# A cross-attention prologue re-ordered: query projections moved into the first units' steps, loads re-sequenced, key transfers on a second queue, feature maps in two pieces

## The chip, the cores and the metric

The kernel runs on one core of a Trainium2 chip. A core has a matrix engine (PE, whose weight loads the profile shows as PEld), a vector engine (DVE), a scalar engine (ACT), a general engine (POOL) and SyncE (SP), which here only issues transfers. Each works through its own instructions in order; semaphores tie them together. PE writes into eight PSUM banks, which DVE and ACT read out. The metric is the device time of one execution in microseconds, smaller is better.

## The reference

One layer over x (4 batches, 256 rows, 256 columns) with a context of 4 x 4096 rows. All in float32:

```python
x = x + xattn(layernorm(x), ctx, ctx)    # 16 heads of 16: softmax(Q K^T / 4) V, then Wh
x = x + attn(layernorm(x))               # causal, features exp(clip(x_n @ omega * sqrt(2s) - s))
x = x + ffn(layernorm(x))                # silu(gate) * up, then down; hidden 768
```

Nearly all the work is the first line: for each of 4 x 16 heads 256 queries meet 4096 keys.

## The kernel before

`cross_attention` works in 16 **units**: a batch and a quad of four heads. A unit has 16 **steps**; a step takes 256 keys. In step n of the main loop (L1116) PE makes transposed scores (`pt`, L856), ACT takes their exponential (`e`, L861), and the product with the values (`pav`, L876) follows one step behind; DVE adds it up (L886). The softmax needs a maximum for each query row first. These come from a second set of scores (`pm`, L810), whose row maxima DVE takes (L817), for the unit after the present one; at a unit's end `shift` (L821) negates the maxima and puts them into a row of the query tile, so that the exponential is taken of shifted scores. Beside this each step makes half a chunk of keys (`pk`, L188) or values (`pv`, L188) for a later unit: `key` and `value` (L736, L763) project 512 context rows. A key chunk leaves PSUM through ACT (`ku`, L753) and is spread by eight small transfers (L756, 16 partitions each) over two of three key tiles `kts`, at rows 32 apart. Those tiles are filled with ones beforehand, since a row of ones meets the shift row.

The first unit has no earlier unit to take its maxima in. The **prologue** (L990 to L1099) makes up for it: it loads weights and context, makes keys 0 to 7 of the first head pairs, values 0 to 3, and runs 16 groups `g` of four `pm` with their maxima, with three more groups for the unit after (`extra`, L1084). `behind` (L1064) says what PE and ACT do after each group. Before it come the queries: `queries(b)` (L939) has a layernorm, a `turn` (four transposes and two copies), for batch 0 a `project` of its first two quads straight into `qT`, and `spread(m)` for half of the quads, which goes through a tile `qu` (L980) and eight transfers on POOL's queue (L983). All of it is done in the prologue for every batch. `qT` is cleared by POOL (L990, L991), and POOL fills the whole of `va`, the later attention's values, with ones (L458). Eleven matmuls of a unit matrix (L1011) stand at the start.

On PE, ACT, DVE and SP the order is the program's own, written out by hand (`manual_schedule`). POOL's order comes from the planner. Each transfer of SP or ACT takes one of eight completion semaphores in turn and waits for the transfer that had it before.

The last unit's steps carry the start of the causal attention (`plan`, L495): `features(n)` (L301) makes a quad's feature maps by PE (`pf`, L309), DVE (clip, L315), ACT (exponential, L316) and POOL (a factor on the key half, L317). `attend` (L321) uses them for masked scores `pa`, their product `po` with `va` and a division. After the last unit a hand-made list (L643 to L672) interleaves the remaining attention with the feed-forward: `hidden(m)` (L576) makes a gate product `pg` and an up product `pu`.

Of the kernel before, what the change touches and what calls it, by code (L numbers as in the profile page):

```python
# [20 lines left out]
P = 128  # L21
# [18 lines left out]
def perceiver_layer(  # L40
# [32 lines left out]
    def load_queries():  # L73

        for to, src, queue in ((bk_sb, bkP, nc.scalar), (bqu_sb, bqP, nc.gpsimd)):
            for q in range(NQ):
                queue.dma_start(
                    out=to[64 * (q % 2) : 64 * (q % 2) + 64, q // 2 : q // 2 + 1],
                    in_=src.rearrange("(j r) q -> j r q", r=32)[:, 1 : 1 + HD, q : q + 1],
                )  # L80
        nc.scalar.dma_start(out=wq_sb, in_=wqP)
        nc.scalar.dma_start(out=bq_sb, in_=bqP)

# [217 lines left out]
    def features(n):  # L301
# [11 lines left out]
        for i, pf in enumerate(pfs):  # L313
            f = feature(n + i // 2, i % 2)
            nc.vector.tensor_scalar(f, pf.rearrange("p s t -> p (s t)"), low, top, ALU.max, ALU.min)  # L315
            nc.scalar.activation(f, f, AF.Exp, bias=shift)  # L316
            nc.gpsimd.tensor_scalar(f[:, T:], f[:, T:], fac, 1.0, ALU.mult, ALU.mult)  # L317

# [125 lines left out]
    def start_causal():  # L444
# [10 lines left out]
        def constants():  # L455


            nc.gpsimd.memset(va, 1.0)  # L458
# [29 lines left out]
        def call(f, *args):  # L488
# [21 lines left out]
            -3: [call(features, 0)],  # L510
            -1: [steps[0][0]],
            0: [steps[0][1], steps[1][0]],
            1: [call(features, 2)],
            2: [steps[1][1], call(qk_normed, 2)],
# [6 lines left out]
            9: [call(features, 4)],  # L521
            10: [project_o],
# [13 lines left out]
        tc, xr, load_x, load_queries, load_rest, ctxT, wq_sb, bq_sb, bqu_sb, wkP, bk_sb, wvP, eps, ident, layernorm, product4,  # L536
# [22 lines left out]
    def feed_forward(b):  # L559
# [15 lines left out]

        def hidden(m):  # L576
            pg, pu = bank([P, 2, T], "pg"), bank([P, 2, T], "pu")
            for ps, w in ((pg, wg), (pu, wu)):
                for i in range(2):
                    ns = slice((2 * m + i) * P, (2 * m + i + 1) * P)  # L580
                    for k in range(KC):
                        nc.tensor.matmul(  # L582
                            ps[:, i, :], lhsT=w[:, k, ns], rhs=zT[:, k, :], start=k == 0, stop=k == KC - 1
                        )
            th = work.tile([P, 2, T], F32, tag="th", name="th")
            nc.scalar.activation(th, pg, AF.Tanh, scale=0.5)
            nc.vector.scalar_tensor_tensor(th, th, 1.0, pg, ALU.add, ALU.mult)
            nc.vector.tensor_tensor(hT[:, 2 * m : 2 * m + 2, :], pu, th, ALU.mult)
# [18 lines left out]
        return norm, turn, hidden, down  # L607

    with tc.manual_schedule(engines={ET.PE, ET.Activation, ET.DVE, ET.SP}):
# [52 lines left out]
        for n in range(NQ, NB + 1):  # L662
            if n > NQ + 1:
                steps[n - 1][1]()
            if NQ < n < NB:
                steps[n][0]()
            for piece in first.get(n, []):
                piece()
# [6 lines left out]
def cross_attention(tc, xr, load_x, load_queries, load_rest, ctxT, wq_sb, bq_sb, bqu_sb, wkP, bk_sb, wvP, eps,  # L675
# [17 lines left out]
    nc = tc.nc  # L693
    NU = B * NQ
# [3 lines left out]
    with ExitStack() as st:  # L698
# [15 lines left out]
        ones = big.tile([P, 1], F32, tag="ones", name="ones")  # L714

# [223 lines left out]
        def queries(b):  # L939
# [7 lines left out]
            def turn():  # L947
# [3 lines left out]
                for i in range(2):  # L951
# [3 lines left out]
                    nc.scalar.copy(  # L955
# [4 lines left out]
            def project():  # L960

                for i in range(2):
                    ps = bank([P, T], "pq")
                    for k in range(KC):
# [3 lines left out]
                    nc.scalar.activation(  # L968
                        qT[:, i, b * T : (b + 1) * T], ps, AF.Identity, bias=bq_sb[:, i : i + 1]
# [19 lines left out]

        nc.gpsimd.memset(qT[:, 2:, :T], 0.0)  # L990
        nc.gpsimd.memset(qT[:, :, T:], 0.0)  # L991
        with tc.manual_schedule(engines={ET.PE, ET.Activation, ET.DVE, ET.SP}):
            nc.sync.dma_start(out=wk, in_=wkP.rearrange("p k (h r) -> p k h r", r=32))
            for b in range(1, B):
                load_context()
                load_x(b)
            nc.sync.dma_start(out=wv, in_=wvP)

# [3 lines left out]
            load_queries()  # L1002
            nc.vector.tensor_reduce(ones, ident.rearrange("p (j r) -> p r j", r=32)[:, 0, :], AX.X, ALU.add)

            def fill(kt, c0, c1, engine=nc.vector):
                engine.tensor_copy(kt[:, c0 * CH : c1 * CH], ones.to_broadcast([P, (c1 - c0) * CH]))


            warm = bank([P, P], "warm")
            for _ in range(11):  # L1010
                nc.tensor.matmul(warm, lhsT=ident, rhs=ident, start=True, stop=True)  # L1011
# [7 lines left out]
            for i in range(2):  # L1019
                fill(kts[i], 0, 2)  # L1020
            normal = [q[0]() for q in qs]
            for piece in normal[0]:
                piece()
            headed(wk, wk_sb)
            qs[0][1]()
            for i in range(2):
                fill(kts[i], 2, NCH)
            normal[1][0]()
            whole(key(0, 0, (nc.sync, nc.scalar) * 2 + (nc.sync,) * 4))
            qs[0][2]()  # L1030
            for piece in normal[1][1:]:
                piece()
# [3 lines left out]
            nc.vector.memset(neg0, 0.0)  # L1036
            whole(key(0, 1))
            wqu = wide.tile([P, KC, 2 * D], F32, tag="wk", name="wqu")
            headed(wq_sb.rearrange("p k (h r) -> p k h r", r=32), wqu[:, :, :D])
            for k in range(KC):  # L1040
                nc.scalar.copy(
                    wv_sb[:, k, :].rearrange("p (h d) -> p h d", d=HD),
                    wv[:, k, : H * (HD + 1)].rearrange("p (h e) -> p h e", e=HD + 1)[:, :, :HD],
                )

            def filled(c):
                return lambda: nc.scalar.copy(
                    kts[2][:, 2 * c * CH : 2 * (c + 1) * CH], ones.to_broadcast([P, 2 * CH])
                )

            def keys(c):
                return lambda: whole(key(0, c))
# [174 lines left out]
```

## Time and profile before

| | |
|---|---|
| median of three runs | 1184.65 us (1183.34 to 1185.9) |
| the profiled execution | 1184.44 us |
| its span, first to last instruction | 1182.7 us |
| granted PE clock over the span | 0.997 |
| PE busy | 1171.0 us (99%) |
| DVE busy | 904.8 us (77%) |
| ACT busy | 696.5 us (59%) |
| POOL busy | 236.8 us (20%) |
| chain that ended last, by engine | PE 97%, DVE 2%, ACT 1% |
| DVE row maxima L817 | 1024, 683 ns each, 634.9 us |
| query transfers L983 on POOL | 56, 486 ns an issue, 3.7 us to landing |

The span is the time between the first and the last instruction of the program; the execution's time is a little longer. An engine's busy time is the union of its instructions. In the timeline and the groups, a row names the line, the operation, `out<-in`, the shapes and how many instructions it merges; float32 matmuls appear as two records each, so 16 `pk` matmuls are 32 records. In square brackets stands the engine's idle time before the row and what released it. PE's matmuls overlap in the array, so a run's length is best read from the start of one run to the start of the next.

### The profile page before, as it was taken

The page shows a single profiled execution, that of the slowest core. Times are in us where ns is not written, and L with a number is a line of the kernel's source. Part 1 is how long each engine was busy: PE and PEld are TensorE (multiplying, and loading weights), DVE is VectorE, ACT ScalarE, POOL GpSimd, SP SyncE. Part 2 cuts the span into 40 slices and gives each one's busy share as a digit, 9 for nine tenths or more (in the row PEclk, how much of TensorE's full clock was granted, in tenths as well). Part 3 has the DMA queues.
Part 4 walks back from the last instruction along what each step waited for, and adds up shares of the span by engine and source line. Part 5 has one row for each costly group of instructions (what it writes and reads, how often), then busy time and mean ns, then how long its engine had stood idle before and what let it go on. Part 6 is the DMA issues. An engine that isn't in the chain of part 4 may idle for free.

```text
span 1182.7 us, 42980 instructions
## 1 busy us (share of the span) xinstructions
PE 1171.0 (99%) x18024; PEld 798.5 (68%) x18024; DVE 904.8 (77%) x1723; ACT 696.5 (59%) x1444; POOL 236.8 (20%) x443
## 2 busy tenths in 40 slices
PE   8999999999999999999999999999999999999998
PEld 4476667766776677667766776667666666667777
DVE  7987787777777777877777877798887788567753
ACT  4456666666666655666666665666664456876442
POOL 3730302011111212120202020303031132213210
PEclk8999999999999999999999999999999999999999
DMA  6562442234223432333224322432233112000000
GB/s 211 145 208 66 115 121 81 61 103 114 85 78 87 118 96 74 81 111 101 83 76 117 93 80 75 113 113 83 66 105 111 39 42 69 11 2 10 10 11 18
DMA packets 55160, 99.99 MB, mean 85 GB/s; under 512 B 23392, under 2 KB 28056, under 8 KB 54968
## 3 DMA queue, kind: packets, MB, share of 16 engines
q1 hardware_dynamic: 44904, 91.84, 26.2%
q0 software_dynamic: 9440, 4.81, 2.1%
q8 instruction: 143, 2.34, 0.8%
q10 hardware_dynamic: 624, 0.59, 0.2%
q14 instruction: 49, 0.40, 0.1%
HBM read 76.13 MB, written 3.21 MB: 67 GB/s over the span
## 4 chain that ended last, share of the span: by engine, by line
PE 97%; DVE 2%; ACT 1%; issue 0%; POOL 0%; ACTq 0%; POOLq 0%
PE pt L856 23%; PE pm L810 19%; PE pav L876 19%; PE pv L188 11%; PE pk L188 11%; PE pg L582 2%; PE pd L598 2%; PE pu L582 2%; PE pa L335 1%; PE pqk L188 1%; PE po L361 1%; DVE mx L817 1%; PE py L409 1%; PE pf L309 1%; PE py L188 1%; PE pa L340 1%
## 5 line engine op out<-in xcount | busy, mean ns | idle before, releaser
L861 ACT ACTIVATE e<-pt 128x512 f32<-128x512 f32 x1024 | 529.3, 602 | 374.4 <-PE pm L810 356.6
L817 DVE TENSOR_REDUCE mx<-pm 128x1 f32<-128x512 f32 x1024 | 634.9, 683 | 127.0 <-PE pm L810 126.7
L856 PE MATMUL pt<-qa,kt 32*128 32x256 f32 x4096 | 501.4, 388 | 0.7 <-DVE qa L842 0.5
L810 PE MATMUL pm<-kt,qT 32*128 32x512 f32 x2048 | 498.4, 617 | 0.1
L856 PEld LDWEIGHTS pt<-qa,kt 32*128 32x128 f32 x4096 | 318.0, 184 | 124.0 <-ACT v L781 42.4
L876 PE MATMUL pav<-e,v 128*32 128x256 f32 x4096 | 269.1, 380 | 0.0
L810 PEld LDWEIGHTS pm<-kt,qT 32*128 32x128 f32 x2048 | 181.3, 191 | 15.7 <-DVE mx L817 4.9
L876 PEld LDWEIGHTS pav<-e,v 128*32 128x32 f32 x4096 | 128.5, 110 | 74.0 <-issue 4.6
L886 DVE TENSOR_TENSOR av<-pav,av 128x256 f32<-128x256 f32 x240 | 101.6, 423 | 57.8 <-PE pav L876 57.3
L188 PE MATMUL pv<-wv_sb,wff 128*32 128x128 f32 x4096 | 137.3, 276 | 0.0
L188 PE MATMUL pk<-wff,wk_sb 128*32 128x256 f32 x2048 | 137.1, 389 | 0.0
L188 PEld LDWEIGHTS pv<-wv_sb,wff 128*32 128x32 f32 x4096 | 104.3, 109 | 43.1 <-DVE mx L817 43.1
L188 PEld LDWEIGHTS pk<-wff,wk_sb 128*32 128x32 f32 x2048 | 54.7, 110 | 66.6 <-DVE mx L817 38.8
L925 POOL TENSOR_TENSOR oT<-oT,bvT 128x64 f32<-128x64 f32 x32 | 8.6, 290 | 357.8 <-DVE oT L922 356.2
L908 POOL DMA_DIRECT2D oT<-scr x112 | 66.5, 626 | 22.1 <-DMA scr<-av 19.0
L753 ACT ACTIVATE ku<-pk,bk_sb 128x256 f32<-128x256 f32 x128 | 63.2, 495 | 12.6 <-PE pk L188 11.1
L832 POOL DMA_DIRECT2D qa<-neg x60 | 33.1, 564 | 133.8 <-DVE neg L829 96.3
L781 ACT COPY v<-pv 128x256 f32<-128x256 f32 x128 | 51.3, 401 | 9.7 <-PE pv L188 9.7
L352 DVE TENSOR_TENSOR at<-pa,mask 128x384 f32<-128x384 f32 x34 | 17.3, 551 | 19.5 <-PE pa L340 19.5
L983 POOL DMA_DIRECT2D qT<-qu x56 | 26.8, 486 | 14.6 <-ACT qu L980 11.1
L316 ACT ACTIVATE kt<-kt,shift 128x512 f32<-128x512 f32 x32 | 22.3, 727 | 8.4 <-DVE kt L315 8.4
L315 DVE TENSOR_SCALAR kt<-pf,low,top 128x512 f32<-128x512 f32 x32 | 23.7, 803 | 4.4 <-PE pf L309 4.3
(146 smaller groups left out, 645.3 us busy)
## 6 DMA issues: line engine op xcount, KB each, us to landing
wff<-in_ctxT_dram SPq DMA_DIRECT2D x128, 512.0 KB
kt<-ku SPq DMA_DIRECT2D x510, 32.0 KB
scr<-av POOLq DMA_DIRECT2D x14, 128.0 KB, 2.1
oT<-scr POOLq DMA_DIRECT2D x112, 8.0 KB, 2.7
xr<-in_x_dram SPq DMA_DIRECT2D x4, 256.0 KB
out_dram<-o SPq DMA_DIRECT2D x8, 128.0 KB
qa<-neg POOLq DMA_DIRECT2D x60, 1.0 KB, 3.5
qT<-qu POOLq DMA_DIRECT2D x56, 16.0 KB, 3.7
```

Source lines behind the costliest of these rows:

```text
L188: nc.tensor.matmul(out[js], lhsT=lhsT[:, js], rhs=rhs, **flags)
L582: nc.tensor.matmul(ps[:, i, :], lhsT=w[:, k, ns], rhs=zT[:, k, :], start=k == 0, stop=k == KC - 1)
L753: nc.scalar.activation(ku[:, cs], made.pop(), AF.Identity, bias=bk_sb[:, m : m + 1])
L781: nc.scalar.copy(to.rearrange("p t (h d) -> p t h d", d=HD + 1)[:, :, :, :HD], made.pop().rearrange("p t (h d) -> p t h d", d=HD),)
L810: nc.tensor.matmul(pm, lhsT=qT[rows, q, ts], rhs=kt[rows, c * CH : (c + 1) * CH], start=True, stop=True,)
L817: nc.vector.tensor_reduce(mx[:, i, j, c : c + 1], pm, AX.X, ALU.max)
L832: nc.gpsimd.dma_start(out=qa[32 * j : 32 * j + 1, :].rearrange("o (p i) -> o p i", i=2), in_=neg[:, j, :])
L856: nc.tensor.matmul(pt[:, i, :], lhsT=kt[rows, ks], rhs=qa[rows, :], start=True, stop=True)
L861: nc.scalar.activation(e, pt, AF.Exp, scale=0.25)
L876: nc.tensor.matmul(pav[32 * h : 32 * h + 32, :], lhsT=v[:, t % KT, c0 : c0 + 32], rhs=es[n, h][:, i, :], start=i == 0, stop=i == 1,)
L886: nc.vector.tensor_tensor(avs[u], pav, avs[u], ALU.add)
L908: queue.dma_start(out=oT[:, k, q % 2, j], in_=scr[32 * j : 32 * j + HD, k * P : (k + 1) * P].rearrange("e (r a) -> r e a", a=16),)
```

## The change

In the prologue:

- The transfers are issued in another order and on other queues. wq goes from ACT's queue to SP's. Of x and the context only what the first two key chunks use stands ahead of the first keys' transfers; x of batches 2 and 3, the value weights and later context chunks follow between the key chunks. Keys 2 to 7 put two of their eight transfers on POOL's queue.
- POOL no longer clears `qT`; ACT copies a column of zeros into it in pieces. DVE fills the key tiles with ones only for chunks 0 to 3; ACT fills the rest. `va` gets its ones by two DVE memsets of its columns of ones, in the step where POOL's memset stood in the plan.
- Batch 0's transposed layernorm and its first queries are read out by DVE instead of ACT. Twelve matmuls of the unit matrix stand at the start, and six more after key chunk 1.
- The statistics of batches 2 and 3 move by a group, and `behind` is dealt out anew; values 0 to 3 follow groups 11 to 14.

In the main loop, the second half of batch 0's queries and the turns and both halves of batches 1 to 3 stand after steps 1, 3 to 5, 7 to 9 and 17 to 19. `att0` takes its buffer when it is first used, since the query weights keep that buffer until then.

In the causal part, `features` becomes `feature_arguments` (PE, DVE) and `feature_exps` (ACT, POOL); in the plan of the last unit the second piece comes a step later. In the end phase one gate product is made ahead of the last unit's division.

```diff
@@ -70,16 +70,27 @@
     bk_sb, bqu_sb = (const.tile([P, KC], F32, tag=name, name=name) for name in ("bk_sb", "bqu_sb"))
-    def load_queries():
...
-        nc.scalar.dma_start(out=wq_sb, in_=wqP)
+    def load_biases():
+        load_spread(bk_sb, bkP, nc.scalar)
         nc.scalar.dma_start(out=bq_sb, in_=bqP)
+    def load_spread(to, src, queue):
...
+    def load_weights():
+        nc.sync.dma_start(out=wq_sb, in_=wqP)
+    def load_later():
+        nc.vector.memset(bqu_sb, 0.0)
+        load_spread(bqu_sb, bqP, nc.gpsimd)
+    loads = load_x, load_biases, load_weights, load_later
     bvT = const.tile([P, H], F32, tag="bvT", name="bvT")
...
@@ -298,7 +309,7 @@
         i = 2 * (n % 4) + part
         return kts[2 if n % 8 < 4 else 0][:, i * 2 * T : (i + 1) * 2 * T]
-    def features(n):
+    def feature_arguments(n):
         b, q = divmod(n, NQ)
         cs = slice(b * T, (b + 1) * T)
@@ -311,10 +322,19 @@
                     start=True, stop=True,
                 )
         for i, pf in enumerate(pfs):
+            nc.vector.tensor_scalar(
+                feature(n + i // 2, i % 2), pf.rearrange("p s t -> p (s t)"), low, top, ALU.max, ALU.min
+            )
+    def feature_exps(n):
+        for i in range(4):
             f = feature(n + i // 2, i % 2)
-            nc.vector.tensor_scalar(f, pf.rearrange("p s t -> p (s t)"), low, top, ALU.max, ALU.min)
             nc.scalar.activation(f, f, AF.Exp, bias=shift)
             nc.gpsimd.tensor_scalar(f[:, T:], f[:, T:], fac, 1.0, ALU.mult, ALU.mult)
+    def features(n):
+        feature_arguments(n)
+        feature_exps(n)
     got, place = [], {}
...
@@ -455,7 +475,8 @@
         def constants():
-            nc.gpsimd.memset(va, 1.0)
+            nc.vector.memset(va[:, :, : H * (HD + 1)].rearrange("p t (h e) -> p t h e", e=HD + 1)[:, :, :, HD], 1.0)
+            nc.vector.memset(va[:, :, H * (HD + 1) :], 1.0)
             nc.vector.tensor_scalar(top, rest[6], 20.0, None, ALU.add)
             nc.vector.tensor_scalar(low, rest[6], -20.0, None, ALU.add)
             nc.vector.tensor_scalar(shift, rest[6], -1.0, None, ALU.mult)
...
@@ -507,19 +528,20 @@
...
-            -3: [call(features, 0)],
+            -3: [call(feature_arguments, 0)],
+            -2: [call(feature_exps, 0)],
             -1: [steps[0][0]],
             0: [steps[0][1], steps[1][0]],
-            1: [call(features, 2)],
-            2: [steps[1][1], call(qk_normed, 2)],
+            1: [call(feature_arguments, 2)],
+            2: [call(feature_exps, 2), steps[1][1], call(qk_normed, 2)],
             3: [steps[1][2], steps[2][0]],
...
-            9: [call(features, 4)],
-            10: [project_o],
+            9: [call(feature_arguments, 4)],
+            10: [call(feature_exps, 4), project_o],
...
@@ -573,15 +595,25 @@
                     nc.tensor.transpose(ps[:, k, j, :], z[:, j, k * P : (k + 1) * P], ident)
             nc.scalar.copy(zT.rearrange("p k (j t) -> p k j t", t=P), ps)
+        gates = {}
+        def half(m, name, w):
...
+            return ps
+        def gate(m):
+            gates[m] = half(m, "pg", wg)
         def hidden(m):
-            pg, pu = bank([P, 2, T], "pg"), bank([P, 2, T], "pu")
...
+            if m not in gates:
+                gate(m)
+            pg, pu = gates[m], half(m, "pu", wu)
...
@@ -664,6 +696,8 @@
                 steps[n - 1][1]()
             if NQ < n < NB:
                 steps[n][0]()
+            if n == NB:
+                ff[2][4](2)
             for piece in first.get(n, []):
                 piece()
             if n > NQ and n % 2 == 0:
...
@@ -952,7 +988,7 @@
                     ps = bank([P, KC, P], "tr")
                     for k in range(KC):
                         nc.tensor.transpose(ps[:, k, :], z[:, i, k * P : (k + 1) * P], ident)
-                    nc.scalar.copy(
+                    (nc.vector.tensor_copy if b == 0 else nc.scalar.copy)(
                         zT.rearrange("p k (r a) -> p k a r", a=16)[:, :, 8 * i : 8 * i + 8],
                         ps.rearrange("p k (a r) -> p k a r", r=16),
                     )
@@ -965,8 +1001,8 @@
                         product4(
                             ps, wq_sb[:, k, i * P : (i + 1) * P], got[0][:, k, :], start=k == 0, stop=k == KC - 1
                         )
-                    nc.scalar.activation(
-                        qT[:, i, b * T : (b + 1) * T], ps, AF.Identity, bias=bq_sb[:, i : i + 1]
+                    nc.vector.tensor_scalar(
+                        qT[:, i, b * T : (b + 1) * T], ps, bq_sb[:, i : i + 1], None, ALU.add
                     )
             def spread(m):
...
@@ -986,29 +1022,34 @@
             return norm, turn, project, spread
-        nc.gpsimd.memset(qT[:, 2:, :T], 0.0)
-        nc.gpsimd.memset(qT[:, :, T:], 0.0)
         with tc.manual_schedule(engines={ET.PE, ET.Activation, ET.DVE, ET.SP}):
             nc.sync.dma_start(out=wk, in_=wkP.rearrange("p k (h r) -> p k h r", r=32))
-            for b in range(1, B):
-                load_context()
-                load_x(b)
-            nc.sync.dma_start(out=wv, in_=wvP)
+            load_context()
             tmp = small.tile([P, 1], F32, tag="first", name="first")
             nc.scalar.activation(tmp, eps, AF.Sqrt)
-            load_queries()
+            load_biases()
+            load_weights()
+            load_x(1)
             nc.vector.tensor_reduce(ones, ident.rearrange("p (j r) -> p r j", r=32)[:, 0, :], AX.X, ALU.add)
-            def fill(kt, c0, c1, engine=nc.vector):
-                engine.tensor_copy(kt[:, c0 * CH : c1 * CH], ones.to_broadcast([P, (c1 - c0) * CH]))
-            warm = bank([P, P], "warm")
-            for _ in range(11):
-                nc.tensor.matmul(warm, lhsT=ident, rhs=ident, start=True, stop=True)
+            def fill(kt, c0, copy=nc.vector.tensor_copy):
+                copy(kt[:, c0 * CH : (c0 + 2) * CH], ones.to_broadcast([P, 2 * CH]))
+            def clear(b, q0=0):
+                nc.scalar.copy(
+                    qT[:, q0:, b * T : (b + 1) * T], zero.unsqueeze(2).to_broadcast([P, NQ - q0, T])
+                )
+            def warm(n):
+                ps = bank([P, P], "warm")
+                for _ in range(n):
+                    nc.tensor.matmul(ps, lhsT=ident, rhs=ident, start=True, stop=True)
+            warm(12)
             def headed(src, to):
...
@@ -1017,39 +1058,49 @@
             qs = [queries(b) for b in range(B)]
             for i in range(2):
-                fill(kts[i], 0, 2)
+                fill(kts[i], 0)
             normal = [q[0]() for q in qs]
             for piece in normal[0]:
                 piece()
+            load_later()
             headed(wk, wk_sb)
             qs[0][1]()
-            for i in range(2):
-                fill(kts[i], 2, NCH)
-            normal[1][0]()
-            whole(key(0, 0, (nc.sync, nc.scalar) * 2 + (nc.sync,) * 4))
-            qs[0][2]()
-            for piece in normal[1][1:]:
-                piece()
+            nc.vector.memset(zero, 0.0)
             flat = vs.rearrange("p c t v -> p (c t) v")
             nc.vector.memset(flat[:, :, : 8 * (HD + 1)].rearrange("p t (h e) -> p t h e", e=HD + 1)[:, :, :, HD], 1.0)
             nc.vector.memset(flat[:, :, 8 * (HD + 1) :], 1.0)
             nc.vector.memset(neg0, 0.0)
+            for i in range(2):
+                fill(kts[i], 2)
+            whole(key(0, 0, (nc.sync, nc.scalar) * 2 + (nc.sync,) * 4))
+            load_context()
+            load_x(2)
+            qs[0][2]()
+            for piece in normal[1]:
+                piece()
             whole(key(0, 1))
+            warm(6)
+            load_context()
+            nc.sync.dma_start(out=wv, in_=wvP)
+            load_x(3)
             wqu = wide.tile([P, KC, 2 * D], F32, tag="wk", name="wqu")
             headed(wq_sb.rearrange("p k (h r) -> p k h r", r=32), wqu[:, :, :D])
...
-            def filled(c):
-                return lambda: nc.scalar.copy(
-                    kts[2][:, 2 * c * CH : 2 * (c + 1) * CH], ones.to_broadcast([P, 2 * CH])
-                )
+            def values_headed():
+                for k in range(KC):
+                    nc.scalar.copy(
+                        wv_sb[:, k, :].rearrange("p (h d) -> p h d", d=HD),
+                        wv[:, k, : H * (HD + 1)].rearrange("p (h e) -> p h e", e=HD + 1)[:, :, :HD],
+                    )
+            def filled(i, c):
+                return lambda: fill(kts[i], c, nc.scalar.copy)
+            def cleared(*args):
+                return lambda: clear(*args)
             def keys(c):
-                return lambda: whole(key(0, c))
+                return lambda: whole(key(0, c, ((nc.sync,) * 3 + (nc.gpsimd,)) * 2))
             def values(c):
                 return lambda: whole(value(0, c))
...
@@ -1062,25 +1113,25 @@
             behind = [
-                [keys(2), turned(1)],
-                [keys(3), filled(0)],
-                [queried(1, 0), queried(1, 1)],
-                [keys(4), filled(1)],
-                [queried(0, 1), turned(2)],
+                [],
+                [keys(2)],
+                [keys(3), cleared(1)],
+                [filled(0, 4), filled(1, 4)],
+                [keys(4), cleared(0, 2)],
+                [cleared(2), filled(0, 6)],
                 [keys(5)],
-                [queried(2, 0), queried(2, 1)],
-                [keys(6), filled(2)],
-                [turned(3), queried(3, 0)],
+                [filled(1, 6), cleared(3)],
+                [keys(6), values_headed],
+                [filled(2, 2)],
                 [keys(7)],
-                [queried(3, 1)],
-                [values(0), filled(3)],
+                [filled(2, 4), values(0)],
+                [filled(2, 6), values(1)],
+                [filled(2, 0), values(2)],
+                [values(3)],
                 [],
-                [values(1)],
-                [],
-                [values(2), values(3)],
             ]
-            parts = dict(zip((0, 1, 2, 5, 6, 7), (*normal[2], *normal[3])))
+            parts = dict(zip((1, 2, 3, 5, 6, 7), (*normal[2], *normal[3])))
             extra = {1: 0, 3: 1, 5: 2}
             for g in range(NS):
                 products, reduce = maxima(g, range(4))
...
@@ -1101,12 +1152,21 @@
             for t in range(NT):
                 nc.gpsimd.tensor_tensor(xr[:, t, :], xr[:, t, :], rest[2], ALU.add)
-            later = {}
+            later = {1: queried(0, 1)}
+            for b, n in ((1, 3), (2, 7), (3, 17)):
+                later.update({n: turned(b), n + 1: queried(b, 0), n + 2: queried(b, 1)})
             plan = {}
             masks(wide.tile([P, KC, VW], F32, tag="wv", name="mask").rearrange("p k v -> p (k v)")[:, : 3 * P].rearrange(
                 "p (i t) -> p i t", t=P))
-            att0 = wide.tile([P, KC, 2 * D], F32, tag="wk", name="att0")
-            place["att"] = lambda b: att0[:, :, :D]
+            att0 = []
+            def place_att(b):
+                if not att0:
+                    att0.append(wide.tile([P, KC, 2 * D], F32, tag="wk", name="att0"))
+                return att0[0][:, :, :D]
+            place["att"] = place_att
             place["at"] = lambda: upool.tile([P, CH], F32, tag="ku", name="at")[:, : 3 * P].rearrange("p (i t) -> p i t", t=P)
             place["avT"] = lambda: upool.tile([P, T], F32, tag="qu", name="avT")
             place["oT"] = lambda: upool.tile([P, T], F32, tag="qu", name="oT").rearrange("p (k t) -> p k t", t=P)
```

## The prediction, made before the result was known

> **What bounds it now.** I read the busy time by stretches first, then the order of events in the front, then the matmul rows of one steady step.
>
> ```profile
> 0.00:5.00 5.00, 3.11 (x14) 3.11 (x15) 3.10 (x3) 1.49 (x2) 4.36 (x10) 1.00 0.65 182
> 5.00:10.00 5.00, 1.38 (x12) 1.18 (x10) 4.53 (x9) 0.92 (x3) 4.50 (x5) 0.84 0.97 297
> 10.00:15.00 5.00, 5.00 (x44) 2.37 (x46) 4.32 (x6) 2.02 (x4) 0.00 (x0) 0.50 1.06 365
> ...
> 20.82:73.02 52.20, 51.22 (x708) 26.75 (x696) 47.67 (x85) 21.02 (x45) 28.14 (x60) 1.00 0.54 157
> ...
> 80.21:141.17 60.96, 60.96 (x1000) 41.33 (x996) 46.50 (x82) 38.04 (x81) 9.32 (x15) 1.00 0.39 118
> ```
>
> Columns: stretch, length, busy PE, PEld, DVE, ACT, POOL (instructions), granted PE clock, DMA share, GB/s. From 80.21 on, PE is busy every microsecond of a unit while DVE has 46.50 of 60.96 and ACT 38.04: there PE work costs its full length. Between 20.82 and 73.02 DVE works 47.67 of 52.20; its waits in that stretch put all 4.3 us of idle time before a row maximum (L817) down to the matmul (L810) it reads. There DVE is the near limit and PE has slack behind it.
>
> ```profile
> 2.07 5.49 DVE L1006 COPY kt<-ones 128x1024 f32<-128x1024 f32 x2
> ...
> 7.47 0.41 DVE L119 BATCH_NORM_STATS2 ln_st<-xr 128x6 f32<-128x256 f32 x1
> ...
> 9.71 1.12 PE L954 MATMUL tr<-ident,z 128*128 128x128 f32 x4 [3.62 <-DVE z L131]
> ...
> 10.75 3.64 PE L188 MATMUL pk<-wff,wk_sb 128*32 128x256 f32 x32
> ...
> 14.17 2.44 PE L188 MATMUL pq<-zT,wq_sb 128*32 128x256 f32 x32
> ...
> 18.26 1.80 PE L810 MATMUL pm<-kt,qT 32*128 32x512 f32 x8
> ...
> 20.82 2.45 DVE L817 TENSOR_REDUCE mx<-pm 128x1 f32<-128x512 f32 x4
> ...
> 73.04 0.22 DVE L826 TENSOR_REDUCE neg<-mx 128x8 f32<-128x64 f32 x1
> ```
>
> This is the timeline (start, length): the layernorm waits for two slow fills, PE idles 3.62 us, its clock falls to 0.50, and the first keys take 3.64 us where the same 32 records later take 1.93. The first maxima start at 20.82, their last consumer at 73.04.
>
> **Front, part by part.** *POOL memsets of qT and va gone; second fill shortened.* The fill of 1024 elements took 2782 ns each beside POOL's 2.65 us memset (L991) and its DMA issues, while that of 3072 took 1746 ns with POOL quiet, so 0.58 us per 1024. The fills then end near 2.8. The next limit is x: the fourth load on SP waits for x(0) to land and starts at 3.55. Statistics 3.6, then the present 2.24 us to the transposes: 5.9. The first warm-up matmuls, 12 x 0.38 us (L1011: 22 records in 4.19), from 1.4, end at 6.0. PE is never idle for long, so I take full clock.
>
> [...] Rows for the POOL route: 486 ns an issue and 3.7 us to landing, beside 0.62 us an issue on SP (8 in 4.95). Keys 2 to 7 put 2 of 8 on POOL; SP saves 1.2 us, the row lands about as soon. Both give 0 for the end.
>
> *Loads in order of need.* wq moves from ACT's queue to SP's; x(2), x(3), wv wait behind the first keys' DMAs. Up to the second context 2.62 MB are needed. The rows above moved 0.91 MB by 5.0; at 297 to 365 GB/s the rest takes 4.7 to 5.8 us, plus some 0.9 to signal (wk's bytes fit in that by 4.7, its waiter ran at 5.64): 10.6 to 11.7, I take 11.2. The first context (1.31 MB) is there at 7.3.
>
> *The chain to the first maxima.* Key 0: 7.4 to 9.3 (1.86 a key at full clock); ku 0.47, at 9.8. ACT issues two key rows at 1.1 us each (2.20 now), last at 12.0, landed at 13.7. pq 9.3 to 11.2, its bias now added on DVE (2 x 0.42), no longer behind ACT's issues. Key 1: 11.3 to 13.2. Six more warm-up matmuls, 6 x 0.33 = 2.0: 15.2. **First pm at 15.2** instead of 18.26. Added DVE work (zT 2 x 0.5, small memsets, the stats of x(1)) is done by 14.5, because DVE has no maxima yet. Bounds: 14.2 with the best DMA rate; 17.3 if key 0 and pq run at half clock again (1.7 + 0.6 more).
>
> *From there to the shift.* DVE: 76 maxima at 0.602 (9.65 us for 16) = 45.7; statistics of x(2), x(3) 2 x 1.05, roots 2 x 0.32: 48.5. PE has 19 groups of pm x 1.08 = 20.5, six keys x 1.86 = 11.2, four values x 1.89 = 7.6: 39.3, against 48.1 today with seven pqu halves and three turns. I walked the eight PSUM banks through the new order: DVE waits 1.1 for the first group, 0.3 in the middle and 0.5 to 0.6 before each of the last three groups, where values now stand in four neighbouring steps and PE needs 1.9 + 1.08 = 3.0 against DVE's 2.41. Sum 51.8; shift at 67.0 instead of 73.0: **-6.0**. ACT's new fills and clears (8 and 3.5 x 1.04) total 12.1 where L1047 had 4.1; ACT is at 21.02 of 52.20, so hidden; uncovered, each would hold a key's bank for 1 us. SP's loads behind six key issues (0.68 each) start at 14; the third context lands about 17, needed at 17.4; if late, DVE's 2.4 us per queued group covers it.
>
> **The steps.** Seven query halves and three turns go where PE has no slack.
>
> ```profile
> 858.45 1.05 PE L876 MATMUL pav<-e,v 128*32 128x256 f32 x16
> 859.31 1.05 PE L188 MATMUL py<-wh_sb,oT 128*32 128x256 f32 x16
> ...
> 938.87 1.08 PE L188 MATMUL pv<-wv_sb,wff 128*32 128x128 f32 x32
> 939.88 0.66 PE L232 MATMUL tr<-ident,z 128*128 128x128 f32 x4
> 940.47 1.07 PE L876 MATMUL pav<-e,v 128*32 128x256 f32 x16
> ```
>
> py has the form of a query half, 16 records of 128x256. Its step goes from pav at 858.45 to pav at 863.12, 4.67 us; its neighbour from 854.64 to 858.45, 3.81. So a half costs 0.86, and a turn 0.70 (the step with L232 is 4.52). 7 x 0.86 + 3 x 0.70 = **+8.1**. ACT (0.47 and 1.0 added to 2.9 in a 3.81 us step) and DVE fit. POOL issues 56 DMAs x 0.49 = 27 us over 20 steps; before the second unit's shift at step 13 only 40 of them, 20 us from step 1, and finish(0)'s reads precede the last 16. Rows for units 2 and 3 are read from step 13. Nothing waits: 0, at most 1 us if a shift's four issues stand behind eight queries' (3.9 us).
>
> **Features and gate.** The chain of waits leaves PE for ACT once:
>
> ```profile
> 1003.60 1.16 ACT kt L316 x2
> ...
> 1005.37 0.59 ACT e L861
> ...
> 1006.00 1.13 PE pt L856 x10
> ```
>
> The exponentials of the features stand before a step's own e; split, e goes first. ACT has 9.06 busy of 10 us there (9.51 in the next feature stretch), and the scores of the following step now wait for the later features, so of the 2.4 us on ACT I take **-0.6** back over three pieces; bounds 0.5 worse, 2 better. A gate product fills PE's wait for avT before the last division (pt_o 1.00 instead of 0.66): **-0.3**. va's memsets on DVE fall in a step with some 0.9 us to spare: 0.
>
> **Sum.** -6.0 + 8.1 - 0.6 - 0.3 = +1.2. The profiled execution took 1184.44 (span 1182.7 and 1.7 around it), 0.2 under the median of the three runs: **1185.6**.
>
> **Rivals.** *The front shortens more (faster).* pm at 13.9 with loads at 365 GB/s and shorter warm-ups, DVE waits of 1.1 only, 2 us from the features: 13.9 + 49.6 = 63.5, -9.5 + 8.1 - 2.3 = -3.7: 1180.7. For it: 350 to 405 GB/s between 8 and 15 us; against: PE's excess in the last four groups.
>
> *The clock stays low (slower).* PE waits for the first context after 6.6 and for the second after 11.2. If either gap, or few matmuls in it, halves the clock as at 10 to 15 us now, the first pm comes at 17.3 and one more key at half clock adds 1.8: 19.1 + 51.8 = 70.9, -2.1 + 8.1 - 0.9 = +5.1: 1189.5. It decides above a first pm of about 16.5. Against it: gaps under 1 us here, 3.62 before.
>
> *A queue takes the gain (slower).* SP now has loads between keys 0 and 1, and keys' rows 3 and 7 come through POOL. If rows land 2.4 us late once (one DVE group), +3.6: 1188.0. Against: keys have 9 us from ku to use.
>
> *The steps hide the queries* (PE not the bound): then -6.9, 1177.5; the full PE row of 60.96 speaks against it, under 2%.
>
> **How the numbers follow.** Forecast 0.52, with its own range 1183 to 1188; faster rivals 0.22, clock 0.16, queue 0.10. What a measurement tells from no change is 0.2%, 2.4 us: below 1182.3 or above 1187.0. Faster 0.19 + 0.03 of the forecast; slower 0.25 of the slow rivals + 0.13; the rest same. Range 1180.7 to 1189.5, both outer rivals' times.
>
> **What will show it.** First pm near 15.2, fills near 0.6 us, granted clock 1.00 throughout; the negated maxima near 67; steps 1, 5, 8, 9 at 4.7 us instead of 3.81, step 3 near 4.5, first units together +8.1; ACT's e ahead of the kt exponentials; a longer front than 52 us from first pm, or steps unchanged where queries stand, would make it wrong.

## The result, and the profile after

The changed kernel takes **1191.7 us** (median of six runs, 1190.56 to 1195.68) where the kernel before takes 1184.36 beside it: a ratio of 1.0066 with a 95% interval of 1.0056 to 1.0076, so 7.3 us slower. The profiled execution took 1191.42, its span is 1189.7 against 1182.7.

Where the 7.0 us of span come from is read from the starts of the products with the values (`pav`), which mark the units (the last line begins where the last run of `pav` does):

| stretch | before | changed | difference |
|---|---|---|---|
| start to the first maxima's negation | 73.04 | 69.54 | -3.5 |
| from there to the first `pav` | 7.17 | 8.65 | +1.5 |
| units 0 and 1 | 121.96 | 129.99 | +8.0 |
| units 2 to 13 | 753.56 | 753.56 | 0 |
| units 14 and 15 | 105.06 | 106.93 | +1.9 |
| the rest, to the end of the span | 121.91 | 121.03 | -0.9 |

Only the first line has a gain of size. The busy time by stretches of the changed kernel (stretch, length, busy PE, PEld, DVE, ACT and POOL with their instructions, granted PE clock, DMA share, GB/s):

```profile
0.00:5.00 5.00, 3.54 (x16) 3.54 (x17) 2.56 (x7) 1.76 (x3) 0.73 (x7) 1.00 0.56 166
5.00:10.00 5.00, 4.21 (x51) 3.47 (x53) 3.62 (x12) 1.23 (x4) 2.66 (x4) 1.00 0.97 338
10.00:15.00 5.00, 5.00 (x76) 3.28 (x68) 2.78 (x9) 1.69 (x4) 0.00 (x0) 1.00 0.29 71
16.24:69.54 53.30, 46.78 (x592) 23.88 (x588) 48.65 (x89) 24.02 (x42) 6.79 (x15) 0.94 0.60 179
69.54:78.19 8.65, 7.86 (x114) 5.97 (x118) 4.88 (x9) 4.12 (x9) 5.21 (x8) 0.80 0.94 300
...
78.19:144.79 66.60, 66.60 (x1088) 44.84 (x1084) 46.67 (x82) 42.48 (x91) 23.58 (x49) 1.00 0.30 86
```

The clock between 10 and 15 us is 1.00 where it was 0.50: the early part went as meant. But from the first row maxima to their negation PE now works only 46.78 of 53.30 us, at a mean clock of 0.94, and in the 8.65 us behind it at 0.80. The first unit is full of matrix work and 5.6 us longer.

The timeline of the changed kernel, prologue only (start, length, engine, line, operation, idle time before it and what ended it; SPq is SP's queue of transfers):

```profile
1.64 1.29 DVE L1038 COPY kt<-ones 128x1024 f32<-128x1024 f32 x2
...
3.52 0.43 DVE L130 BATCH_NORM_STATS2 ln_st<-xr 128x6 f32<-128x256 f32 x1 [0.59 <-DMA xr<-in_x_dram]
...
8.04 1.93 PE L199 MATMUL pk<-wff,wk_sb 128*32 128x256 f32 x32 [0.79 <-DMA wff<-in_ctxT_dram]
...
15.08 2.01 PE L846 MATMUL pm<-kt,qT 32*128 32x512 f32 x16
...
16.24 2.48 DVE L853 TENSOR_REDUCE mx<-pm 128x1 f32<-128x512 f32 x4 [2.19 <-PE pm L846]
...
21.97 0.43 SPq L1084 DMA_DIRECT2D wv<-in_wvP_dram  x1
22.45 0.43 SPq L58 DMA_DIRECT2D xr<-in_x_dram  x1
22.98 0.41 SPq L765 DMA_DIRECT2D wff<-in_ctxT_dram  x1
23.50 3.68 SPq L792 DMA_DIRECT2D kt<-ku  x6
...
30.54 2.54 PE L846 MATMUL pm<-kt,qT 32*128 32x512 f32 x8 [1.95 <-DMA kt<-ku]
...
33.02 3.64 PE L199 MATMUL pk<-wff,wk_sb 128*32 128x256 f32 x32
...
38.06 2.48 DVE L853 TENSOR_REDUCE mx<-pm 128x1 f32<-128x512 f32 x4 [1.89 <-PE pm L846]
...
69.54 0.22 DVE L862 TENSOR_REDUCE neg<-mx 128x8 f32<-128x64 f32 x1
...
69.81 0.44 PE L875 MATMUL pn<-ident,neg 128*128 128x128 f32 x2 [2.81 <-DVE neg L862]
```

The fills take 1.29 us for two, the statistics begin at 3.52, the first score matmuls at 15.08 and the first maxima at 16.24. Then three things are new. At 30.54 PE has stood 1.95 us for the rows of key 2. The next key takes 3.64 us instead of 1.93, and DVE waits 1.89 us for the group behind it. And before the first shift PE stands idle for 2.81 us, because the last group has nothing behind it any more: values 2 and 3, which stood there, moved up.

### The profile page after: what moved, and what is told of

Its sections match the earlier page's. It is cut to its first block, busy times and chain, and to the rows that moved or that the text cites. A ratio compares the mean times of both kernels' runs of the same rounds, so it can differ in the third digit from the quotient of the medians.

```text
span 1189.7 us, 43026 instructions
## 1 busy us (share of the span) xinstructions
PE 1174.0 (99%) x18038; PEld 802.5 (67%) x18038; DVE 901.5 (76%) x1731; ACT 702.9 (59%) x1448; POOL 236.2 (20%) x452
## 4 chain that ended last, share of the span: by engine, by line
PE 95%; DVE 1%; ACT 0%; issue 0%; DVEq 0%; ACTq 0%
PE pt L892 23%; PE pav L912 19%; PE pm L846 19%; PE pv L199 11%; PE pk L199 10%; PE pg L605 2%; PE pd L630 2%; PE pu L605 2%; PE pa L355 1%; PE pqk L199 1%; PE po L381 1%; PE pf L320 1%; PE py L429 1%; PE py L199 1%; PE pa L360 1%; PE pqu L199 1%
## 5 line engine op out<-in xcount | busy, mean ns | idle before, releaser
L199 PEld LDWEIGHTS pv<-wv_sb,wff 128*32 128x32 f32 x4096 | 104.6, 110 | 44.3 <-DVE mx L853 43.5
```

The source lines that it names most:

```text
L199: nc.tensor.matmul(out[js], lhsT=lhsT[:, js], rhs=rhs, **flags)
```

## The experiments

Ratios are to the kernel before, with a 95% interval. Each time is a median; the kernel before gave 1184.32 to 1184.48 beside runs 1 to 8.

**1. Key 2's rows ahead of the loads.** The rows of key 2 are issued at 23.50 behind four loads (context, value weights, x, context). Three of these loads were put behind the rows:

```diff
             whole(key(0, 1))
             warm(6)
-            load_context()
-            nc.sync.dma_start(out=wv, in_=wvP)
-            load_x(3)
...
-                [keys(2)],
+                [keys(2), later_loads],
```

> The changed kernel, with the value weights, x of batch 3 and the context of key chunk 5 issued behind key chunk 2's rows instead of ahead of them. Theory (late rows): in the changed kernel the matrix engine stood 1.95 us at 30.54 for key 2's rows, then ran the next key at half clock (3.64 instead of 1.93 us), and DVE idled 0.17 + 1.89 us for it. With the rows issued about 1.6 us sooner and fewer bytes ahead of them that wait goes, the negated maxima come near 67.5 instead of 69.54, and the time falls by 2.0 us to about 1189.7. Rival (POOL's two transfers are the late ones): the wait stays, time within 0.4 of the changed kernel's 1191.7.

Measured: 1189.98 us, ratio 1.0045 (1.0033 to 1.0057); the negated maxima at 67.78. By stretches:

```profile
16.46:67.78 51.32, 46.17 (x592) 23.69 (x587) 48.45 (x89) 23.78 (x41) 6.82 (x15) 1.00 0.62 186
67.78:76.42 8.64, 7.85 (x114) 5.93 (x118) 4.88 (x9) 4.12 (x9) 4.93 (x8) 0.80 0.85 293
```

The clock is 1.00 up to the negation, the stretch is 2.0 us shorter, and the 8.64 us behind it are as in the changed kernel: the late rows and the pause in front of the shift are two separate losses. What is left of DVE's idle time, 51.32 - 48.45 = 2.9, lies mostly ahead of the last four groups (0.58, 0.47, 0.48, 0.48); the forecast had 0.5 to 0.6 ahead of the last three.

The expectation gave two reasons, sooner issues and fewer bytes ahead. The first did not come about. The first two lines and the stretch from the rows' first issue to PE's use of them (29.35) are of this run; the last line is the changed kernel's from its first row issue on:

```profile
24.22 4.27 SPq L792 DMA_DIRECT2D kt<-ku  x6
28.28 3.45 PE L846 MATMUL pm<-kt,qT 32*128 32x512 f32 x16 [0.41 <-ACT qT L1042]
...
24.20:29.35 5.15, 4.74 (x55) 1.67 (x49) 5.12 (x12) 3.00 (x6) 0.96 (x2) 1.00 0.59 155
...
23.50:27.00 3.50, 3.50 (x44) 1.56 (x40) 3.50 (x7) 1.54 (x3) 0.31 (x1) 1.00 1.05 358
```

The six rows were issued from 24.22 to 28.49, later than the 23.50 to 27.18 of the changed kernel, and yet the second of the two groups at 28.28, which reads key 2, begins without a pause. So it was not the time of issue that made the rows late but the bytes of the loads issued ahead of them: with those, the DMA engines' share was 1.05 while the rows were issued, without them 0.59. The wait is no chance of one execution: in the profiles of the changed kernel and of runs 2, 3, 4 and 8, which all have the loads ahead, PE stands 1.95 to 3.37 us at this place, in runs 1 and 5 not at all.

**2. POOL's transfers taken away.** All eight rows of keys 2 to 7 go to SP.

```diff
-                return lambda: whole(key(0, c, ((nc.sync,) * 3 + (nc.gpsimd,)) * 2))
+                return lambda: whole(key(0, c))
```

> The changed kernel with all eight transfers of keys 2 to 7 on SP's queue. Rival (POOL's transfers are the late ones): the wait of 1.95 us for key 2's rows goes, time about 1189.7. Theory (rows stand behind the loads on SP): the wait stays or grows by up to the 1.2 us that two more issues take, time 1191.7 to 1193.

Measured: 1196.6 us (1192.31 to 1197.84), ratio 1.0099 (1.0084 to 1.0114). The rival falls: a wait of 2.19 us stays at the same place (31.02). But it was dearer than the theory's upper end as well. Timeline:

```profile
62.87 1.95 SPq L765 DMA_DIRECT2D wff<-in_ctxT_dram  x4
...
66.82 2.43 PE L199 MATMUL pv<-wv_sb,wff 128*32 128x128 f32 x64 [2.44 <-DMA wff<-in_ctxT_dram]
...
71.30 2.48 DVE L853 TENSOR_REDUCE mx<-pm 128x1 f32<-128x512 f32 x4 [4.41 <-PE pm L846]
```

With two more issues a key, SP comes to the contexts of the values at 62.87 instead of 58.80. PE waits 2.44 us for one, and the last group's maxima 4.41. So the second queue, which the forecast priced at nothing, is worth 4.9 us to this order of work by the medians (3.9 by the means of six runs each, which scatter). In this prologue the time to issue counts for what stands behind: six rows take 3.68 us to issue in the changed kernel, and the contexts of the values come 4.07 us later when SP has eight to issue.

**3. A filler behind the last group.** The pause of 2.81 us is filled with matmuls that nobody reads:

```diff
                 [values(3)],
-                [],
+                [lambda: warm(9)],
```

> The changed kernel with nine matmuls of the unit matrix behind the last group, where the matrix engine has nothing to do for 2.81 us before the first shift. Theory (the clock): that pause lets the granted clock fall to 0.50 in the first unit's first steps; filled, the clock stays at 1.00, the stretch from the negated maxima to the first product with the values falls from 8.65 us to the 7.17 of the kernel before, and the time by 1.5 us to about 1190.2. Rival (the first steps are slow from the loads that fill the DMA engines there, 340 to 386 GB/s): no change, 1191.7.

Measured: 1190.18 us, ratio 1.0052 (1.004 to 1.0064). By stretches, from the negation to the first `pav`, and two microseconds of it:

```profile
69.67:76.94 7.27, 6.38 (x114) 5.21 (x118) 4.94 (x10) 3.94 (x9) 3.29 (x5) 1.00 0.93 278
72.00:74.00 2.00, 2.00 (x51) 1.43 (x43) 1.82 (x4) 1.74 (x4) 0.34 (x1) 1.00 0.79 299
```

8.65 becomes 7.27 at a clock of 1.00, with the transfers still at 0.93 of the DMA engines' time. So the clock it was, not the loads. In the changed kernel the same two microseconds have 0.50:

```profile
72.00:74.00 2.00, 2.00 (x20) 1.13 (x16) 1.29 (x2) 1.08 (x2) 1.02 (x2) 0.50 0.97 386
```

**4. Features in one piece again.**

```diff
-            -3: [call(feature_arguments, 0)],
-            -2: [call(feature_exps, 0)],
+            -3: [call(features, 0)],
...
```

and the same for quads 2 and 4.

> The changed kernel with the features in one piece again, as in the kernel before. Theory (the split costs): units 14 and 15 lose the 1.87 us that they gained in length, time about 1189.8. Rival (the split gains, as forecast, and the longer units come from elsewhere, for instance from the moved memset of va): 1191.7 to 1192.3.

Measured: 1190.93 us (1189.22 to 1191.2), ratio 1.0052 (1.004 to 1.0064). Units 14 and 15 are back at 60.31 and 44.73, 1.89 us less than in the changed kernel. The moved memsets of `va` are still in this kernel, so they are not the cause. The whole time shows less of it, because in the profiled execution the front was 1.3 us longer: PE's wait at the place of key 2's rows was 3.37 us instead of 1.95. What the split did is seen in the changed kernel's timeline around the first and the second of the three feature pieces:

```profile
1011.78 2.57 ACT L332 ACTIVATE kt<-kt,shift 128x512 f32<-128x512 f32 x4
...
1013.16 0.70 PE L355 MATMUL pa<-kt 64*128 64x256 f32 x4 [0.92 <-POOL kt L333]
...
1014.23 2.07 ACT L897 ACTIVATE e<-pt 128x512 f32<-128x512 f32 x4
...
1014.89 1.07 PE L912 MATMUL pav<-e,v 128*32 128x256 f32 x16 [0.16 <-ACT e L897]
...
1030.05 0.44 PE L397 MATMUL pt_o<-ident,avT 128*128 128x128 f32 x2 [1.47 <-ACT avT L387]
```

The four exponentials still stand ahead of an `e`, only of the following step's. Moved a step later they are also right ahead of their own consumers: PE waits 0.92 us for the last factor on POOL, and where a division follows it waits 1.47 us for an `avT` copy that ACT takes behind them.

**5. The three repairs together.** Rows first, filler and features whole; the queries stay in the steps.

> The changed kernel with three repairs together: key 2's rows ahead of the loads, nine filler matmuls behind the last group, features in one piece; the queries stay in the first units' steps. Theory (the three losses are separate and add up): 2.0 + 1.4 + 1.9 = 5.3 us below the changed kernel, about 1186.2, so that the rest, the eight us that the queries cost in the steps, is still not earned by the front: within 0.3% of the kernel before. Rival (the losses hide each other, a later wait takes up what one repair frees): 1188 to 1190.

Measured: 1186.76 us (13 runs), ratio 1.0022 (1.0014 to 1.003). The three losses add up, to within 0.6 us of the 1186.2 expected. With them gone the changed kernel still is slower than the one before. What is left should be the move of the queries itself, and the next two runs try that.

**6. The queries back in the prologue.** As 5, `behind` dealt out with the turns and query halves between the groups, values 2 and 3 behind the last.

```diff
-            later = {1: queried(0, 1)}
...
+            later = {}
...
+                [filled(1, 6), cleared(3), turned(2), queried(2, 0)],
...
+                [values(2), values(3)],
```

> As the repaired kernel, but the seven query halves and three turns stand between the prologue's groups again, and values 2 and 3 behind the last group in place of the filler. Theory (in the prologue the vector engine is the limit, so that the matrix engine takes the queries there nearly for nothing, while a step pays them in full): the first two units go back to 60.96 and 61.0 us, 8.0 less; the front grows by at most 2 us; time 1178.5 to 1181. Rival (the prologue's matrix engine is full too): the front grows by 6 to 8 us, time about 1185 to 1186.

Measured: 1184.39 us, ratio 1.0002 (0.9994 to 1.001). Units 0 and 1 went back to 60.96 and 61.0, but the first `pav` came at 80.97, 4.65 later than in 5. The time lies between the theory's and the rival's, and the timeline shows a third reason:

```profile
42.80 0.66 PE L989 MATMUL tr<-ident,z 128*128 128x128 f32 x4
...
44.18 1.03 ACT L1037 COPY kt<-ones 128x1024 f32<-128x1024 f32 x1
...
45.12 1.04 ACT L1041 COPY qT<-zero 128x1024 f32<-128x1024 f32 x1
...
46.06 1.00 ACT L990 COPY zT<-tr 128x256 f32<-128x256 f32 x2
...
47.12 1.94 PE L199 MATMUL pqu<-zT,wqu 128*32 128x256 f32 x16 [3.66 <-ACT zT L990]
```

The transposes were done at 43.5, but ACT had a fill and a clear of 1.03 and 1.04 us ahead of the copies, and the query half stood right behind the turn on PE. PE waited 3.66 us, and the next row maxima 5.55. This was a mistake in dealing out, which run 9 mends.

**7. The move of the queries alone.** The kernel before, with only the seven halves and three turns moved to the same steps.

```diff
-                [keys(2), turned(1)],
+                [keys(2)],
...
-            later = {}
+            later = {1: queried(0, 1)}
+            for b, n in ((1, 3), (2, 7), (3, 17)):
+                later.update({n: turned(b), n + 1: queried(b, 0), n + 2: queried(b, 1)})
```

> The kernel before with one thing of the change alone: the seven query halves and three turns moved from the prologue into the steps. Theory (vector engine is the prologue's limit): units 0 and 1 grow by 8.0 us, the front falls only by what DVE waited for the matrix engine, 2 to 4 of 4.3 us: time 1188.5 to 1190.5. Rival (the matrix engine sets the prologue): the front falls by 7 to 8 us, time within 1 us of 1184.5.

Measured: 1188.01 us (1187.11 to 1188.24), ratio 1.0028 (1.0017 to 1.0039). By stretches, from the first maxima to their negation and the first unit:

```profile
19.66:68.43 48.77, 48.77 (x596) 26.43 (x592) 47.18 (x85) 14.88 (x31) 1.30 (x4) 1.00 0.52 149
75.60:142.20 66.60, 66.60 (x1089) 44.82 (x1083) 46.51 (x82) 42.41 (x90) 28.40 (x55) 1.00 0.42 118
```

The prologue is now DVE's: 47.18 of 48.77 us. PE is recorded as busy throughout too, but of the two it is PE that waits: in that stretch the weight loads of `pm` wait 10.5 us in all for DVE's maxima, the maxima 1.7 us for `pm` (total, times, longest).

```profile
PEld pm L810 <- DVE mx L817: 10.5, 33, 0.8
...
DVE mx L817 <- PE pm L810: 1.7, 3, 1.0
```

The first `pav` comes at 75.60, so the front gave 4.6 us, a little over what the theory allowed, because the first maxima also came 1.2 us sooner (19.66 for 20.82). The steps took 8.0. The move alone costs 3.4 us of front against steps, 3.7 by the times.

**8. Without the gate product ahead.**

```diff
-            if n == NB:
-                ff[2][4](2)
```

> The changed kernel without the gate product made ahead of the last division. By the comparison of the traces after the last product with the values, 121.91 us before and 121.03 changed, the gate gives 0.88: time about 1192.6. By the forecast's term it gives 0.3: about 1192.0.

Measured: 1193.16 us, ratio 1.0075 (1.0062 to 1.0088); the intervals overlap with the changed kernel's. The trace decides: from the start of the last run of `po` to the start of the last sum DVE writes (`o`) it takes 29.11 us, in the changed kernel 28.82, before 29.12. The gate is worth 0.3. The other 0.6 us of the last table line lie behind that, where the outputs land (3.05 us to the span's end instead of 3.63). They are there without the gate too; their cause was not tried.

**9. Everything that proved good.** As 6, the query pieces spread over groups 0, 2, 3, 5, 7, 9, 11 and 13, no query half right behind its turn, and `qT` cleared by DVE ahead of the first maxima:

```diff
+            nc.vector.memset(qT[:, 2:, :T], 0.0)
+            nc.vector.memset(qT[:, :, T:], 0.0)
             whole(key(0, 1))
...
+                [keys(3), queried(0, 1)],
+                [queried(1, 0), filled(0, 4), filled(1, 4)],
+                [keys(4)],
+                [turned(2), queried(1, 1), filled(0, 6)],
...
```

> As the run with the queries back in the prologue, dealt out anew: query pieces spread over groups 0, 2, 3, 5, 7, 9, 11 and 13 with a turn always ahead of ACT's fills and never right before its own query half; the query tile cleared by DVE ahead of the first row maximum, where DVE waits 2 us, instead of by ACT. Theory (DVE's 48.5 us of work from the first maxima on are the limit, the earlier run lost 5.55 us in one wait for a turn): negated maxima at 66 to 68, first product with the values at 73.5 to 75.5 instead of 80.21, units 0 and 1 at 61.0, time 1177.5 to 1179.5, faster than both kernels. Rival (queries and values together fill the matrix engine of the prologue): front within 2 us of the kernel before, time 1182 to 1184.5.

Measured: **1178.91 us** (1178.36 to 1180.68) beside 1183.34 (1183.19 to 1185.84) of the kernel before, ratio 0.9956 (0.9943 to 0.997): faster than both. By stretches, from DVE's clear of `qT` to the negation, from there to the first `pav`, and the first unit:

```profile
15.35:69.21 53.86, 53.36 (x692) 26.44 (x696) 51.05 (x90) 26.17 (x52) 33.91 (x72) 0.97 0.66 186
69.21:77.12 7.91, 7.39 (x154) 5.95 (x150) 4.93 (x9) 5.96 (x12) 0.00 (x0) 1.00 0.63 122
77.12:138.08 60.96, 60.96 (x1000) 41.35 (x996) 46.48 (x82) 38.01 (x81) 9.31 (x15) 1.00 0.39 120
```

PE and DVE are both full in the prologue, 53.36 and 51.05 of 53.86. The time is as expected, but the front is later than expected by 1.6 to 3.6 us (77.12 for 73.5 to 75.5). The profiled execution was the slowest of the five (1180.68), and in it the clock fell to 0.50 from 20.86 to 24.28; the median one ran at a mean clock of 1.00. In part the clear is to blame: it took 2.62 us from 15.35, and held the first maxima to 17.89 where PE had work for them by 16.4. Between runs 5 and 9 the spans differ by 7.2 us (1186.1 and 1178.9): the front is 0.8 longer in 9, the first two units 8.0 shorter. That is what the place of the queries is worth, with the new deal and DVE's clear counted in.

## Why the prediction was wrong

The forecast was 1185.6; the profiled execution took 1191.42. Its terms one by one:

- **The first score matmuls at 15.2 at full clock: right** (15.08; 1.00 from 10 to 15 us), as were the fills (0.65 us each for "near 0.6"). The place is in part luck: key 0 began at 8.04 for 7.4, and the six warm-up matmuls behind key 1 then held PE for 1.5 us instead of 2.0.
- **"Shift at 67.0": wrong by 2.5 us.** DVE's work was right (48.65 measured, 48.5 forecast), and the waits ahead of the last four groups too. What failed is the sentence that keys have 9 us from `ku` to use. Key 2's `ku` was there at 20.9 and its rows were needed at 28.6, so it had 7.7, and it took 9.6: 2.6 to the end of key 1's rows and the issue of four loads on SP, 3.7 for six row issues, and 3.4 more until PE could start. Run 1 shows which part was too long: with three of the loads behind the rows, these were issued later and still came in time, so it is what the DMA engines had to move ahead of them (a share of 1.05 while the rows were issued, 0.59 in run 1). The rival of the queue had this mechanism, "rows land late once", but weighed it at 0.10 and forgot the second half: with the pause of 1.95 us the clock went to 0.50, from 30.44 to 37.27 (run 1, without the pause, has 1.00 from 28 to 37). Run 1 takes 2.0 us back; the 0.8 that its shift at 67.78 is still behind 67.0 is mostly small waits of DVE, and the forecast's own items add up to 51.4 to 51.7 us, not the 51.8 that it took.
- **From the shift to the first `pav`, taken over as it was: wrong by 1.5 us.** The forecast counted that values moved away from the last group as cost in the four groups ahead, and not that PE then has nothing to do before the shift. Run 3 shows the clock as the cause: 1.00 for 0.80, and 7.27 us for 8.65.
- **Steps, +8.1: right** (8.03; steps of 4.68 and 4.48 for 4.67 and 4.52). The price from rows of the trace held to 0.04 us a step. POOL's 56 issues cost the steps nothing.
- **Features, -0.6: wrong in sign, +1.9** and outside the bound of 0.5 worse. The forecast named the reason, that scores of the following step wait for the later features, but took the row it could see go (`e` late) and did not walk the step after it, where the consumers on PE and the `avT` copy on ACT stand.
- **Gate, -0.3: right** (0.30).

The three failed terms are 2.5 + 1.5 + 2.5 = 6.5 us; the end of the span gave back 0.6 and left about the 5.8 that the forecast is off. The likeliest case itself, front against steps, was near balance; run 7 shows that the move of the queries by itself stands at +3.7. There the forecast was generous: it gave the front -6.0 for all its causes together, and the run with the three repairs got 3.9 (first `pav` at 76.32 for 80.21). The shift came at 69.05 in that run against 67.78 in run 1, with a wait of 1.93 us for the third context ahead of it (1.36 in the changed kernel); the forecast had that context landing in time.

## What to carry to other kernels

Work moved out of a stretch where two engines are nearly balanced saves only the difference to the other engine, and costs its full length where it lands on an engine without slack (run 7: the front gave 4.6 us, with DVE at 47.18 of 48.77, and the steps took 8.0, with PE at 66.60 of 66.60); so first ask which engine becomes the limit when it is gone. When transfers are put "in order of need", the order must hold the small ones that are made on the way, too: a row that an engine waits for goes ahead of large loads for later, even if it is issued no sooner for it (run 1: 2.0 us), and the time to issue is a resource of its own (run 2: 4.07 us for the contexts behind). And a pause of PE can be dearer than its length (run 3: 1.4 us behind the one of 2.81): leave useful work, or any work, where it would stand idle.

## What the runs showed of the hardware

In the changed kernel the granted clock was 0.50 at two places: for 6.83 us from 30.44, where PE stood 1.95 us up to 30.54, and for 3.41 us from 71.40, behind a pause of 2.81 us up to 69.81. It stayed at 1.00 behind a pause of 1.36 us up to 18.44. But the length of a pause alone does not decide. Two runs show it, run 5 (the first two lines) with a pause of 1.93 us, and run 8 with one of 2.15 (from 16.52 to 18.67), both for the third context:

```profile
18.99 2.45 PE L199 MATMUL pk<-wff,wk_sb 128*32 128x256 f32 x32 [1.93 <-DMA wff<-in_ctxT_dram]
...
20.27:23.69 3.42, 3.42 (x25) 2.11 (x19) 3.00 (x7) 0.98 (x3) 1.01 (x2) 0.50 0.35 107
...
18.67 1.93 PE L199 MATMUL pk<-wff,wk_sb 128*32 128x256 f32 x32 [2.15 <-DMA wff<-in_ctxT_dram]
...
17.97:21.38 3.41, 2.71 (x37) 1.75 (x38) 2.08 (x7) 1.13 (x3) 0.00 (x0) 1.00 0.91 289
21.38:24.79 3.41, 3.41 (x28) 1.55 (x28) 3.41 (x7) 0.00 (x0) 1.01 (x2) 1.00 0.57 131
```

Behind the shorter pause the clock is at 0.50 and the key takes 2.45 us; behind the longer one it stays at 1.00 and the key takes 1.93. And pauses are not the whole of it. In run 9 the clock was 0.50 from 20.86 to 24.28, and of the 15 us from 15.00 to 30.00 PE idled only 0.50, ahead of 18.57. In run 5 the key at 40.35 took 3.31 us, and no idle time of PE is recorded ahead of it from 36.11 on. What decides beside the length of a pause stays open.

By the rows the two pauses of the changed kernel cost about 1.7 and 1.4 us on top of their length (3.64 - 1.93, and 8.65 - 7.27).
